# Three buffers of the fused layers moved to the lowest on-chip addresses

## The chip, the cores and the metric

The kernel runs on one core of a Trainium2 chip. A core has TensorE (PE, matrix products; its loads of stationary operands are listed as PEld), VectorE (DVE), ScalarE (ACT), GpSimd (POOL) and SyncE (SP), each with its own queue of instructions, worked off in order. Tiles live in the on-chip SBUF (128 partitions, so many bytes in each) and, for matrix products, in PSUM. The metric is the time of one execution in microseconds (us); lower is better.

## The reference

Sixteen graphs (batches) of 1024 nodes with 128 features pass through four layers. Each layer's output is added to its input and normalised over the features:

```
x = _layernorm(x + _L0_gnn_ref(x, adj, U))              # mean over neighbours, times U, relu
x = _layernorm(x + _L1_gnn_ref(x, adj, Wv, bv, ...))    # masked attention
x = _layernorm(x + _L2_gnn_ref(x, adj, W, a))           # four-headed graph attention
x = _layernorm(x + _L3_gnn_ref(x, adj, nodemask, ...))  # thinned links, three SAGE layers
```

Layer 3 first thins the links (`_dilate`, row by row), then runs three SAGE layers. Each of these gathers over the thinned links, divides every row by its length, and normalises each feature over all batches and nodes, so no SAGE layer can end before all 16 batches are through it. A linear map of the three results closes the layer.

## The kernel before, in words

`tile_gnn_stack` (L1494) calls two stages, one after the other in the program. A third, `general`, runs only if a flag says that the data is out of the usual, and did not run here.

**`fuse` (L185)** does layers 0 to 2 and the thinning for all batches. Its order of instructions is written by hand: `Loom` interleaves eleven sequences of steps by due times. Each batch's features live in `x0` (L656, three buffers of 4096 bytes a partition). The features are loaded there, all three layers update them in place, and after the last normalisation (`norm.apply`: a chain of small VectorE operations L621 to L635, then eight ScalarE operations L640) one DMA stores them from there to `x3` in DRAM (L1097). Layer 2's output is put together per head: the products `ps_b` (L1060) go through `sums` (L1066) into the totals `every` (L1021), by four VectorE operations (L1070, L1074, L1079, L1080). Then the totals are divided (L1084, L1086) and added to the features (L1089), and the statistics taken (L613). For the last batch this chain from L1070 to L1097 is the end of the stage.

**`sage` (L1111)** does the three SAGE layers and the closing map. Its order is not by hand: the framework orders each engine's instructions by itself, in program order where they are ready by its estimate, with later ones in the gaps. For this it may put `sage` instructions among the last ones of `fuse`. The first SAGE layer works through batches 1, 2, ..., 14, 0, 15, and for the first two of these ("first", "second"):

- `turned` (L1288) loads the features of one batch from `x3` to `xn`, turns them on TensorE (L1295) and copies them to `raw` (L1296, ScalarE).
- `fetch` (L1151) loads the eight blocks of thinned links, one byte an element, to `packed` (tile `ad`, L1155, 12 buffers).
- `weigh` (L1174) multiplies `raw` by the layer's weights `wr` (L1182) and splits the product in `z_hi` (ScalarE, L1184) and `z_lo` (VectorE, L1185).
- `spread_out` (L1158) casts a block of links from one byte to four: blocks 1 and 6 on VectorE (L1162), the six others on ScalarE (L1164), to `links` (12 buffers).
- `count` (L1194) sums the links of each node on TensorE against `ones_bf` (L1199) to `deg_c` (L1203); `degrees` (L1206) sends the sums through DRAM to `deg`; `own` (L1214) uses them.
- `gather` (L1187) is the large product, links by `z_hi` and `z_lo` (L1193). `mix` (L1219, L1222) ends it, with `settle` and `finish` behind.

An `ad` buffer is free for a later batch when its block has been cast and counted.

The weights `wr`, `wx` and vectors of layer 0 are loaded on POOL's queue (`matrix` L48, `column` L53) to the pool `sage_const`, which also holds `ones_bf` (written by VectorE, L1138) and, at its end, `piece`, `once` and `consts`.

**Addresses.** A pool takes a stretch of SBUF in the order in which the pools are opened, and the stretches are given back when a stage ends. So the pools of `sage` lie over those of `fuse`, and what is written first there has to wait until what was there is no longer used. Adding up the tiles (bytes a partition, counted from the start of `fuse_const`):

| pool of `fuse` | from | to | holds, among others |
|---|---|---|---|
| fuse_const | 0 | 6128 | identities, weights of layers 0 to 2 |
| fuse_1 | 6144 | 56576 | `both`, `py`, `ranked`, `qt`, `kt`, `vn`, `every`, `sums` |
| fuse_2 | 56576 | 135168 | `row`, `a`, `x0`, `pr`, `pieces` |
| fuse_3 | 135168 | 172800 | `src` and others, `has` |
| fuse_4 | 172800 | 206592 | `g`, `adt` and others |
| fuse_small | 206592 | 211168 | `ln_st`, `ln_t` and others |

| pool of `sage` | from | to | holds |
|---|---|---|---|
| sage_const | 0 | 7296 | `ones_bf`, weights, `piece`, `once`, `consts` |
| sage_raw | 7296 | 91008 | `raw`, `deg`, `deg_c`, `mf` |
| sage_links | 91008 | 140160 | `links` |
| sage_packed | 140160 | 152448 | `ad` |
| sage_1, sage_2 | 152448 | 207744 | `xn`, `z_hi`, `z_lo`, `own`, `o` and others |

Of the kernel before, what the change touches and what calls it, by code (L numbers as in the profile page):

```python
# [7 lines left out]
F32 = mybir.dt.float32  # L8
# [13 lines left out]
P = 128  # L22
# [162 lines left out]
def fuse(S, ctx, a, x3, adt_d, viol, B=16):  # L185
# [20 lines left out]
    tc, nc = S.tc, S.nc  # L206
# [4 lines left out]
    H, DH = a2.shape[0], a2.shape[1] // 2  # L211
# [4 lines left out]
    D1, GUESS = DH + 1, float(0x5F3759DF) + 3.5 * 2.0**23  # L216
# [3 lines left out]
    dps = ctx.enter_context(tc.tile_pool(name="fuse_dps", bufs=2, space=PSUM))  # L220
    dram = ctx.enter_context(tc.tile_pool(name="fuse_dram", bufs=1, space=DRAM))
    t_d = dram.tile([B, H, N], F32, name="t_d")
    p1 = ctx.enter_context(tc.tile_pool(name="fuse_1", bufs=1))
    p2 = ctx.enter_context(tc.tile_pool(name="fuse_2", bufs=2))
    p3 = ctx.enter_context(tc.tile_pool(name="fuse_3", bufs=3))
# [418 lines left out]
    def flip4(ps, blocks, q):  # L644
        for c in range(4):
            nc.tensor.transpose(ps[:, c, :], blocks(4 * q + c), ident)

    x01 = {}

    def layer0():  # L650
        for b in range(B):
            yield b, "features"
            if b >= 3:
                yield Step(None, 0.0, after=(f"stored {b - 3}",))
            yield Step("SP", 0.2, lag=5.0)
            x0 = x01[b] = p2.tile([P, 8, P], F32, name="x0", bufs=3)  # L656
            nc.sync.dma_start(x0, x_d[b].rearrange("(c p) d -> p c d", p=P))
            py = p1.tile([P, 8, 3 * P + 1], BF16, name="py")
            for q in range(2):
                s = slice(4 * q, 4 * q + 4)  # L660
                yield Step("PE", 0.45, take=[("one", "l0")])
                ps_f = one.tile([P, 4, P], F32, name="ps_f", tag="one")
                flip4(ps_f, lambda c: x0[:, c, :], q)
                yield Step("ACT", 0.47, give=[("one", "l0")])
                xt = p4.tile([P, 4, P], F32, name="xt0", tag="t2k", bufs=3)
                nc.scalar.copy(xt, ps_f)
                yield Step("PE", 0.89, take=[("one", "l0")])
                ps_y = one.tile([P, 4, P], F32, name="ps_y", tag="one")
                for c in range(4):
                    nc.tensor.matmul(ps_y[:, c, :], xt[:, c, :], u_w, start=True, stop=True)  # L670
                yield Step("ACT", 0.47)
                nc.scalar.copy(py[:, s, 0:P], ps_y)
                yield Step("DVE", 0.6, give=[("one", "l0")])
                d = p4.tile([P, 4, P], F32, name="d", tag="t2k", bufs=3)
                V.tensor_tensor(d, ps_y, py[:, s, 0:P], ALU.subtract)
                yield Step("ACT", 0.47)
                nc.scalar.copy(py[:, s, P : 2 * P], d)
                yield Step("DVE", 0.61)
                V.tensor_tensor(py[:, s, 2 * P : 3 * P], d, py[:, s, P : 2 * P], ALU.subtract)
                V.memset(py[:, s, 3 * P : 3 * P + 1], 1.0)  # L680
            yield b, "gather"
            norm = Norm(x0)
            rdeg = sm.tile([P, 8], F32, name="rdeg")
            for p in range(4):
                for k in range(2):
                    ib = 2 * p + k
                    for jb in range(8):
                        if jb % 4 == 0:
                            yield Step(
                                "PE", 0.68, after=(f"has {b} 7", None) if ib + jb == 0 else (),  # L690
                                take=[("one", "l0")] if k + jb == 0 else (),
                            )
                        if k + jb == 0:
                            ps_g = one.tile([P, 2, 256], F32, name="ps_g", tag="one")

                        for q, e in ((2, P + 1), (1, P), (0, P)):
                            nc.tensor.matmul(  # L697
                                ps_g[:, k, 0:e], has[b][:, jb, ib * P : (ib + 1) * P],
                                py[:, jb, q * P : q * P + e],
                                start=(jb == 0 and q == 2), stop=(jb == 7 and q == 0),  # L700
                            )
                s = slice(2 * p, 2 * p + 2)
                yield Step("DVE", 0.1)
                V.reciprocal(rdeg[:, s], ps_g[:, :, P])
                yield Step("ACT", 0.5, give=[("one", "l0")])
                y = p4.tile([P, 2, P], F32, name="y", tag="t2k", bufs=3)
                for k in range(2):
                    nc.scalar.activation(
                        y[:, k, :], ps_g[:, k, 0:P], AF.Relu, scale=rdeg[:, 2 * p + k : 2 * p + k + 1]
                    )  # L710
                yield Step("DVE", 0.86)
                V.tensor_tensor(x0[:, s, :], x0[:, s, :], y, ALU.add)
                norm.take(2 * p)
                norm.take(2 * p + 1)
            yield b, "norm 0"
            yield from norm.apply(f"x1 {b}")
# [295 lines left out]
    def layer2_sums():  # L1012
        for b in each:
            yield b, "sums"
            yield from outputs(b)

    def outputs(b):
        yield Step(None, 0.0, after=(f"bd {b}", f"end {b} 1"))
        x2 = x01.pop(b)
        _, side, pieces, bd = stuff[b]  # L1020
        every_t = p1.tile([P, 8 * H * D1], F32, name="every")  # L1021
        every = every_t.rearrange("p (c h d) -> p c h d", c=8, h=H)
        for jp in range(2):
            for u in range(4):
# [21 lines left out]
        for h in range(H):  # L1046
            for q in range(2):
                for jb in range(8):
                    if jb % 2 == 0:
                        yield Step(  # L1050
                            "PE", 0.72, after=(f"g {b} {h} {q}",), take=[("two", "b")] if q + jb == 0 else (),
                            mark=f"b {b} {h}" if q and jb == 6 else None,
                            give=[("g", (b, h, 0)), ("g", (b, h, 1))] if q and jb == 6 else (),
                        )
                    if q + jb == 0:
                        ps_b = two.tile([P, 2, 512], F32, name="ps_b", tag="two")
                    u, o = jb // 4, jb % 4 * 2 * D1
                    for k in range(4):
                        for t in range(3):
                            nc.tensor.matmul(  # L1060
                                ps_b[:, u, o : o + 2 * D1], side[h, q][:, k, jb * P : (jb + 1) * P],
                                pieces[:, 4 * q + k, :, h, t, :],
                                start=(q == 0 and jb % 4 == 0 and k + t == 0),
                                stop=(q == 1 and jb % 4 == 3 and k == 3 and t == 2),
                            )
            sums = p1.tile([P, 8, 2, D1], F32, name="sums")  # L1066
            up, rest, to = sums[:, :, 0, :], sums[:, :, 1, :], every[:, :, h, :]
            got = ps_b[:, :, 0 : 8 * D1].rearrange("p v (u k d) -> p k v u d", u=4, k=2)
            yield Step("DVE", 0.9, after=(f"b {b} {h}",), give=[("two", "b")])
            V.tensor_tensor(  # L1070
                up.rearrange("p (v u) d -> p v u d", v=2), got[:, 0],
                bd[:, 0, h, :].rearrange("p (v c) -> p v c", v=2).unsqueeze(3).to_broadcast([P, 2, 4, D1]), ALU.mult,
            )
            V.tensor_tensor(  # L1074
                rest.rearrange("p (v u) d -> p v u d", v=2), to.rearrange("p (v u) d -> p v u d", v=2),
                got[:, 1], ALU.subtract,
            )
            yield Step("DVE", 0.9)
            V.tensor_tensor(rest, rest, bd[:, 1, h, :].unsqueeze(2).to_broadcast([P, 8, D1]), ALU.mult)  # L1079
            V.tensor_tensor(to, up, rest, ALU.add)  # L1080
# [23 lines left out]
    with tc.manual_schedule():  # L1104
        loom.run(
            layer2_sums(), sides(), values(), layer2(), scores(), layer1(), layer0(), signs(batches),
            loads(batches), ranks(batches), dilate(batches),
        )
# [1091 lines left out]
```

## Time and profile before

| | us |
|---|---|
| runs of the kernel | 2831.93, 2835.9, 2838.47 (median 2835.9) |
| the profiled execution's own time | 2838.25 |
| its span in the profile | 2836.2 |
| busy in the span | PE 2671.0, PEld 2238.0, ACT 2234.9, DVE 2137.6, POOL 19.5 |

The stage change lies a little after two thirds of the span: the last `ps_b` product of `fuse` ends at 2042.4 us, and the first `ps_g` product of `sage` starts at 2063.7 us. In lines of the timeline the first two numbers are the start and the length in us, then come engine, line, operation, tiles (out <- in), the count, and in brackets the idle time before and what ended it. In lines of waits the numbers are the total in us, how often, and the longest.

### The profile page before, as it was taken

The page shows a single profiled execution, that of the slowest core. Times are in us where ns is not written, and L with a number is a line of the kernel's source. Part 1 is how long each engine was busy: PE and PEld are TensorE (multiplying, and loading weights), DVE is VectorE, ACT ScalarE, POOL GpSimd, SP SyncE. Part 2 cuts the span into 40 slices and gives each one's busy share as a digit, 9 for nine tenths or more (in the row PEclk, how much of TensorE's full clock was granted, in tenths as well). Part 3 has the DMA queues.
Part 4 walks back from the last instruction along what each step waited for, and adds up shares of the span by engine and source line. Part 5 has one row for each costly group of instructions (what it writes and reads, how often), then busy time and mean ns, then how long its engine had stood idle before and what let it go on. Part 6 is the DMA issues. An engine that isn't in the chain of part 4 may idle for free. (4 is left out here: it accounts for less than half of the span.)

```text
span 2836.2 us, 82907 instructions
## 1 busy us (share of the span) xinstructions
PE 2671.0 (94%) x35125; PEld 2238.0 (79%) x35125; DVE 2137.6 (75%) x5704; ACT 2234.9 (79%) x3351; POOL 19.5 (1%) x43
## 2 busy tenths in 40 slices
PE   5999999999999999999999999999799989989997
PEld 4778888888888888888888888877678767767787
DVE  6577777878788786877878687786457768868866
ACT  3788888888888888888888888888666668777625
POOL 1000000000000000000000000000100000000000
PEclk9999999999999999999999999999899989989999
DMA  5111231212303122130312203020355446455368
GB/s 186 44 40 60 63 113 36 95 56 67 106 17 113 39 91 80 43 106 27 109 40 84 94 29 113 24 84 10 92 150 156 146 150 195 137 170 178 117 224 267
DMA packets 225340, 280.26 MB, mean 99 GB/s; under 512 B 18360, under 2 KB 185120, under 8 KB 224960
## 3 DMA queue, kind: packets, MB, share of 16 engines
q1 hardware_dynamic: 223904, 273.69, 30.0%
q8 instruction: 277, 4.54, 0.7%
q0 software_dynamic: 1056, 1.19, 0.2%
q14 instruction: 103, 0.84, 0.1%
HBM read 224.01 MB, written 50.79 MB: 97 GB/s over the span
## 5 line engine op out<-in xcount | busy, mean ns | idle before, releaser
L880 ACT ACTIVATE g<-row,st 128x1024 int8<-128x1024 f32 x512 | 567.1, 1148 | 6.2 <-DMA row<-t_d 6.1
L1060 PE MATMUL ps_b<-pieces,g 128*128 128x66 bf16 x12288 | 422.8, 195 | 2.2 <-DVE g L887 2.2
L1060 PEld LDWEIGHTS <-g 128*128 128x128 fp8e4 x12288 | 403.6, 98 | 4.1 <-DVE g L887 2.3
L1164 ACT CAST links<-ad 128x1024 fp32r<-128x1024 fp8e4 x288 | 290.4, 1047 | 94.3 <-PE ps_g L1193 83.2
L374 DVE TENSOR_TENSOR_SCAN ranked<-has 128x1024 bf16<-128x1024 fp8e4 x128 | 291.6, 2282 | 0.0
L813 PE MATMUL ps_s<-qt,kt 128*128 128x512 f32 x512 | 277.8, 624 | 12.4 <-ACT pr L821 11.8
L456 ACT ACTIVATE x<-both,thr 128x1024 f16<-128x1024 bf16 (+7 forms) x384 | 277.3, 764 | 15.1 <-DVE part L471 8.3
L841 PE MATMUL ps_a<-vn,pr 128*128 128x129 f32 x2048 | 274.1, 281 | 0.0
L1193 PE MATMUL ps_g<-links,z_hi 128*128 128x512 f32 x768 | 260.7, 420 | 0.0
L1193 PE MATMUL ps_g<-links,z_lo 128*128 128x512 f32 x768 | 244.2, 400 | 0.0
L841 PEld LDWEIGHTS ps_a<-vn,pr 128*128 128x128 f32 x2048 | 243.9, 191 | 0.1
L697 PE MATMUL ps_g<-py,has 128*128 128x128 bf16 (+1 forms) x3072 | 205.6, 222 | 0.0
L887 DVE TENSOR_TENSOR g<-g,has 128x1024 int16<-128x1024 int16 x256 | 174.0, 685 | 37.0 <-ACT g L880 37.0
L1032 PE MATMUL ps_m<-pieces,has 128*128 128x132 bf16 x3072 | 196.4, 223 | 5.0 <-ACT pieces L994 3.8
L815 PEld LDWEIGHTS <-has 128*128 128x128 fp8e4 x1024 | 78.7, 98 | 146.0 <-issue 146.0
L1032 PEld LDWEIGHTS <-has 128*128 128x128 fp8e4 x3072 | 188.6, 97 | 6.1 <-issue 5.9
L821 ACT ACTIVATE pr<-ps_s,bound 128x1024 f32<-128x1024 f32 x128 | 141.6, 1106 | 62.0 <-PE ps_s L815 61.7
L697 PEld LDWEIGHTS <-has 128*128 128x128 fp8e4 x3072 | 184.2, 99 | 0.5
L640 ACT ACTIVATE x<-x,ln_t 128x128 f32<-128x128 f32 x384 | 154.6, 486 | 35.8 <-DVE ln_t L635 35.8
L598 ACT ACTIVATE adt<-ps_n 128x512 fp8e4<-128x512 f32 x256 | 152.1, 610 | 27.0 <-PE ps_n L589 23.8
L1193 PEld LDWEIGHTS ps_g<-links,z_lo 128*128 128x128 f32 x768 | 147.0, 192 | 33.1
L561 ACT ACTIVATE x<-ps_r,left 128x512 f16<-128x512 f32 (+1 forms) x192 | 110.2, 581 | 59.4 <-PE ps_r L543 59.0
(295 smaller groups left out, 5524.2 us busy)
## 6 DMA issues: line engine op xcount, KB each, us to landing
a<-in_adj_dram SPq DMA_DIRECT2D x130, 512.0 KB
ad<-adt_d SPq DMA_DIRECT2D x384, 128.0 KB
row<-t_d SPq DMA_DIRECT2D x64, 512.0 KB
row<-rn_d SPq DMA_DIRECT2D x45, 512.0 KB
adt_d<-adt SPq DMA_DIRECT2D x256, 64.0 KB
h_d<-raw SPq DMA_DIRECT2D x32, 512.0 KB
hl<-h_d SPq DMA_DIRECT2D x32, 512.0 KB
x<-in_x_dram SPq DMA_DIRECT2D x16, 512.0 KB
```

Of the source, the lines that this page charges most:

```text
L374: V.tensor_tensor_scan(ranked[c][r], has[c][:, r, :], links[c][:, r, EDGE - 1 : EDGE - 1 + N].bitcast(U8), 0.0, ALU.add, ALU.subtract,)
L456: nc.scalar.activation(x, both[:, at[r] : at[r + 1]], AF.Abs, bias=far[:, r : r + 1], scale=2.0)
L640: nc.scalar.activation(self.y[:, c, :], self.y[:, c, :], AF.Identity, bias=nb[:, c, :], scale=rs[:, c, :])
L697: nc.tensor.matmul(ps_g[:, k, 0:e], has[b][:, jb, ib * P : (ib + 1) * P], py[:, jb, q * P : q * P + e], start=(jb == 0 and q == 2), stop=( ...
L813: nc.tensor.matmul(ps_s[:, u, :], kt[:, at_j], qt[:, f : f + 512], start=True, stop=False)
L841: nc.tensor.matmul(ps_a[:, 0 : P + 1], made[b, i][:, u, ib % 4 * P : (ib % 4 + 1) * P], qkv[b][2][:, i % 4 * 2 + u, :], start=(i % 4 + u = ...
L880: nc.scalar.activation(sg[:, k, :].bitcast(I8), rows[b, h], AF.Sign, bias=st[:, 1, h, ib : ib + 1], scale=-1.0)
L887: V.tensor_tensor(sg.bitcast(I16), sg.bitcast(I16), has[b][:, 2 * q : 2 * q + 2, :].bitcast(I16), ALU.bitwise_and,)
L1032: nc.tensor.matmul(ps_m[:, u // 2, o : o + H * D1], has[b][:, ib, jb * P : (jb + 1) * P], pieces[:, ib, 1, :, t, :], start=(t == 0 and ib ...
L1060: nc.tensor.matmul(ps_b[:, u, o : o + 2 * D1], side[h, q][:, k, jb * P : (jb + 1) * P], pieces[:, 4 * q + k, :, h, t, :], start=(q == 0 an ...
L1164: A.copy(a, t.packed[jb])
L1193: PE.matmul(t.ps[f], z[:, jb, :], t.links[jb][:, halves[f]], start=(jb + i == 0), stop=False)
```

## The change

`x0`, `every` and `sums` get a pool of their own, `fuse_late`, opened ahead of `fuse_1` and so directly behind `fuse_const`. Number and size of their buffers stay (3 x 4096, 4224 and 2112 bytes). No instruction of `fuse` or `sage` is added, taken away or changed.

```diff
     t_d = dram.tile([B, H, N], F32, name="t_d")
+    late = ctx.enter_context(tc.tile_pool(name="fuse_late", bufs=1))
     p1 = ctx.enter_context(tc.tile_pool(name="fuse_1", bufs=1))
     p2 = ctx.enter_context(tc.tile_pool(name="fuse_2", bufs=2))
...
-            x0 = x01[b] = p2.tile([P, 8, P], F32, name="x0", bufs=3)
+            x0 = x01[b] = late.tile([P, 8, P], F32, name="x0", bufs=3)
...
-        every_t = p1.tile([P, 8 * H * D1], F32, name="every")
+        every_t = late.tile([P, 8 * H * D1], F32, name="every")
...
-            sums = p1.tile([P, 8, 2, D1], F32, name="sums")
+            sums = late.tile([P, 8, 2, D1], F32, name="sums")
```

By the same adding up, `fuse_late` lies from 6144 to 24768, `fuse_1` from 24768 to 68864 and `fuse_2` from 68864 to 135168. Everything behind stays where it was, and so do the pools of `sage`.

## The prediction

> **What bounds the kernel now.** The page's first part has PE busy 94% of the span, but the change adds no work and takes none away: it can act only where tiles of `sage` wait for tiles of `fuse`. So I read the stage change, first by windows. The columns are the stretch and its length, then busy us (and instructions) of PE, PEld, DVE, ACT and POOL, then the granted PE clock, the DMA share and GB/s.
>
> ```profile
> 2042.40:2058.00 15.60, 2.99 (x72) 2.65 (x72) 8.23 (x31) 3.25 (x9) 10.01 (x19) 0.62 0.71 211
> 2058.00:2063.70 5.70, 5.14 (x32) 5.12 (x32) 2.48 (x6) 5.55 (x8) 0.00 (x0) 0.55 0.36 94
> 2063.70:2081.00 17.30, 16.06 (x192) 12.44 (x188) 7.69 (x14) 14.35 (x19) 0.00 (x0) 1.00 0.61 177
> 2081.00:2097.00 16.00, 16.00 (x153) 12.79 (x152) 8.95 (x19) 10.25 (x14) 0.00 (x0) 0.89 0.48 132
> 2097.00:2111.40 14.40, 14.40 (x152) 11.51 (x151) 10.94 (x20) 9.24 (x13) 0.00 (x0) 1.00 0.51 157
> ```
>
> From the last `ps_b` product to 2058 PE has 2.99 us of work in 15.60. The first batch's stretch (17.30 us) has PE idle for 1.24 us; the third batch, undisturbed, takes 14.40. Then the timeline of the same place, for who releases whom:
>
> ```profile
> 2047.08 1.64 DVE L613 BATCH_NORM_STATS2 ln_st<-x 128x6 f32<-128x128 f32 x8
> 2047.71 0.55 POOL L48 DMA_DIRECT2D wr<-in_L_gnn_Wr_dram  x1 [2033.45 <-DVE x L1089]
> ...
> 2048.70 0.17 DVE L1138 MEMSET ones_bf<- 128x128 bf16 x1
> 2048.97 1.85 PE L1199 MATMUL ps_d<-ones_bf,ad 128*128 128x1 bf16 x64 [2.69 <-DMA ad<-adt_d]
> 2049.14 0.11 DVE L1472 MEMSET once<- 128x64 uint32 x1
> 2051.22 3.18 ACT L640 ACTIVATE x<-x,ln_t 128x128 f32<-128x128 f32 x8 [13.01 <-DVE ln_t L635]
> 2054.43 0.37 SPq L1097 DMA_DIRECT2D x<-x  x1
> 2057.93 1.07 ACT L1296 COPY raw<-ps_f 128x512 f32<-128x512 f32 x2 [3.53 <-DMA x<-x]
> 2058.15 0.23 DVE L1136 TENSOR_SCALAR mf<-never 128x128 f32<-128x128 f32 x1 [6.97 <-DMA x<-x]
> 2058.72 3.72 PE L1182 MATMUL ps_z<-wr,raw 128*128 128x128 f32 x16
> 2058.89 2.00 ACT L1164 CAST links<-ad 128x1024 fp32r<-128x1024 fp8e4 x2
> 2059.17 0.67 DVE L1162 CAST links<-ad 128x1024 fp32r<-128x1024 fp8e4 x1
> 2062.23 1.48 PE L1295 MATMUL ps_f<-ident,xn 128*128 128x128 f32 x8
> ```
>
> Two rules of the framework can be read here. **Waits go by pool, not by tile**: `mf` lies at byte 89,728, over a buffer of attention weights `pr` (last read by L841 at 1960.5), yet waits for the store of the features `x0`, which shares `fuse_2` with them; and `wr`, at byte 256, over constants, waits for L1089, the last reader of `every` in `fuse_1`, of which `sage_const` covers only bytes 6144 to 7296. **Gaps are filled**: the fills of `ones_bf` and `once` stand inside the last batch's VectorE chain, because they were ready there. Call T0 the landing of the feature store, 2057.9. Today `raw`, `mf` and all `links` start at T0, `wr` and `ones_bf` ten microseconds before it.
>
> **The change part by part.** *Instructions:* none is added or removed, and each tile of `fuse` keeps its number of buffers, so inside `fuse` no wait is new; address alone gets zero. The nearest rows: L1086 writes to `every` in `fuse_1` and L1089 to `x0` in `fuse_2`, both 128x1024 f32 from two inputs, and both took 1.23 us, so an address has no price that shows here.
>
> *`sage_links` (91,008 to 140,160)* lies over `fuse_2` and `fuse_3`. Without `x0` the last users of these are the `ps_b` products, which end at 2042.4, so casts may start there instead of at T0, as blocks land. PE's count of all eight blocks starts at 2048.97, so the last block lands by 2048.9. ScalarE is idle for 13.01 us there: six casts of 1.05 (2.00 for two overlapping) are 6.2 us and fit. This leaves the stretch behind T0 less full: the first batch's stretch is 17.30 against 14.40, so at most 2.9 us can come back. Only 1.24 of these are idle PE, and part of that waits for `ad` blocks whose buffers need the count too. I take 1.7, with ends 0 and 2.9.
>
> *The same casts on VectorE* do harm. Blocks 1 and 6 of the first batch and block 1 of the second (the 12 buffers reach so far) are 0.68 us each. By the gap filling just read they stand inside the chain L1070 to L635, which sets T0 and has no slack: 3 x 0.68 = 2.0 us later. Ends: 0 (they stay behind L635) and 6 (VectorE also stands still till a block lands, see the rivals). On ScalarE casts may push L640 by at most one of 1.05, inside these ends.
>
> *`sage_const` (0 to 7296)* now lies over `fuse_late` (from 6144), by 1152 bytes. By the pool rule all of it, `wr`, `wx` and `ones_bf` too, waits for T0 instead of L1089. The last reader ended at 2047.05 and POOL issued at 2047.71, 0.66 later. How long the load takes:
>
> ```profile
> wr<-in_L_gnn_Wr_dram POOLq DMA_DIRECT2D x3, 64.0 KB, 2.4
> ```
>
> So `wr` is there at T0 + 0.66 + 2.4 = T0 + 3.1, where `ps_z` starts today at 2058.72, T0 + 0.8: 2.3 us later. Behind `wr` on POOL stand the eighteen other loads of weights and vectors, 0.53 each to issue; `wx` and the first vector are needed at the first `mix` and `settle`, 15 us on. `ones_bf` at T0 + 0.3 moves the count (1.85 us of PE) from its free place at 2049 to behind T0, but into the hole in which PE waits for `wr`; the second batch's turn `ps_f` (1.48) may fill the rest. PE's work from T0 to the first `ps_g` is then 1.85 + 3.72 + 1.48 + 0.3 = 7.35 against 5.8 today, so the delay is at least 1.5, and at most 2.3 plus a slow load (the longest of L48's took 4.9, 2.5 more). I take 2.0, ends 1.5 and 4.8. The degree's way through DRAM (L1211, L1212) moves by as much and is needed only at the first `mix`, 15 us on; DVE's `own` waits 2.05 for it already, and the casts queued behind it are done by then.
>
> *`sage_raw`* lies over `fuse_late`, `fuse_1` and `fuse_2` alike: T0 as before. `ad`, `xn`, `z_hi` and the rest lie over pools that do not change. On SP's queue the store L1097 stays behind the same twelve `ad` loads, since a thirteenth needs the count.
>
> **Sum:** +2.0 (chain) +2.0 (weights and count) -1.7 (links) = +2.3 on the profiled execution's 2838.25 (span 2836.2 and 2.05 around it), so 2840.55. That execution lies 2.35 above the median of the runs, 2835.9, so on the median's scale the forecast is 2838.2, 0.08% up. A measurement of this kernel tells about 0.2% (5.7 us) from no change; the three runs alone spread over 6.5.
>
> One rule weighs on this. The granted clock is 0.50 to 0.62 while PE idles before T0 and 1.00 from 2064 on. The Trainium skill (TensorE: Matmul & The Clock Gate, "What's actually happening") has PE at half rate after an idle window of about 3.4 us and at full rate after about as long a busy one. By it the count, now directly ahead of `ps_z`, would begin the warming up earlier, and my 2.0 for weights and count would be nearer 1.5, if the hole for `wr` does not break the window. Another rule speaks for a loss: by SBUF — State Buffer, "SBUF: two separate sides", a copy or cast of VectorE in its two-port mode shuts GpSimd out of a shared port, and so holds up loads issued there. By it each cast of `links` still behind T0 could add its length to the wait for `wr`; no run here shows one.
>
> **The rivals.**
> 1. *The casts come early and nothing pays for them.* If the filled-in casts leave the chain alone and PE has work until `wr` lands, -2.9 + 1.5 remains, or down to -2.9: 2833.0 to 2834.5 on the median's scale. For it: ScalarE's 13.01 us of idling. Against it: `ones_bf` and `once` inside the chain, and the 1152 bytes.
> 2. *VectorE stands still for a block, slower.* The engine's order is fixed; a cast of block 6 put in behind L1084 (2044.5) would hold up the whole chain until the block lands, as late as 2048.9: 4.4, and 2.0 for the casts themselves: +6.4 in place of +2.0, the sum +6.7, so 2842.6. It decides from 3.4 us of standing still (5.7 - 2.3). For it: L1070 to L635 has no slack and blocks land late, PE waited 2.69 for them. Against it: the framework may know this and put the cast behind L613.
> 3. *The change does not do what it says:* some other tile in `fuse_2` or `fuse_3` holds `links` as long as before, and only the price of `sage_const` remains: +2.0, 2837.9. Against it: no reader of these pools after 2042.4 is in the trace.
>
> **How the numbers follow.** Forecast 0.48, rival 1 0.20, rival 2 0.22, rival 3 0.10. The range takes the forecast with its ends (-2.9 + 0 + 1.5 = -1.4, and up to +5 with one slow term), all of rival 1 and most of rival 2 and some of a median's own spread: 2831 to 2844. For faster by over 0.2% nothing reaches -5.7 but a reordering of the whole stage by the framework: 0.07. Slower by over 0.2%: rival 2 and the slow end of the weights, 0.23. Between: 0.70.
>
> **What would show it.** Right: L1164 on ScalarE between 2043 and 2051; L1162 among the operations L1079 to L635, the store's landing some 2 us later; POOL's first L48 and the `ones_bf` fill behind that landing, and PE's `ps_d` count with them; the first batch's stretch nearer 15.5 than 17.3. Wrong: `wr` still loaded at 2047.7, or no cast before T0. A time outside 2831 to 2844 would mean that the order of the whole stage has changed, or that addresses have a price after all.

## The result, and the profile after

The changed kernel's median is 2838.04 us (2833.92 to 2843.2, 21 runs), that of the kernel before, timed beside it, 2832.88 us (2827.36 to 2838.47, 21 runs). The two medians differ by 5.2 us. The ratio, which all comparisons below use, is 1.0016, with a 95% interval of 1.001 to 1.0022: some 4.5 us slower, with 2.8 to 6.2 inside the interval. The profiled execution after took 2840.76 us, its span 2838.9 (before: 2838.25 and 2836.2). Every line number behind the new pool's is one higher than before.

For the comparison I count from the start of the last batch's chain (the last `sums<-ps_b`), called c: 2042.44 before, 2041.37 after. T0 is again the start of `raw`, which the feature store releases. The windows after, cut at the same events as those of before, which the prediction shows (columns: the stretch and its length; busy us of PE, PEld, DVE, ACT and POOL; the granted PE clock; DMA share; GB/s):

```profile
2041.40:2060.80 19.40, 1.25 (x8) 0.86 (x8) 9.75 (x32) 11.81 (x18) 0.00 (x0) 0.59 0.47 141
2060.80:2068.90 8.10, 6.83 (x91) 6.44 (x92) 1.66 (x7) 2.24 (x4) 6.88 (x13) 0.50 0.53 153
2068.90:2084.70 15.80, 15.80 (x193) 13.24 (x192) 7.00 (x12) 9.30 (x12) 3.17 (x6) 1.00 0.68 204
2084.70:2099.10 14.40, 14.40 (x153) 11.68 (x152) 8.71 (x18) 10.80 (x15) 0.00 (x0) 1.00 0.43 123
2099.10:2113.50 14.40, 14.40 (x152) 11.50 (x151) 10.90 (x20) 9.23 (x13) 0.00 (x0) 1.00 0.53 157
```

The chain takes 19.40 us in place of 15.60 (ACT is busy in it for 11.81 in place of 3.25: casts of `links`), T0 to the first `ps_g` 8.10 in place of 5.70 (POOL now works here: the weights), and the next two batches 15.80 and 14.40 in place of 17.30 and 16.00. The first two lines lose 6.2 us, the next two give back 3.1. The third batch's last `mix` ends 72.13 us behind c; before it was 68.95: +3.2. Half of what is given back is the clock's: in the fourth line PE is busy all through in both kernels, but was granted 0.89 before and 1.00 here. The timeline says who waits (... stands for lines left out):

```profile
2041.72 0.42 DVE L1075 TENSOR_TENSOR sums<-every,ps_b 128x264 f32<-128x264 f32 x1
...
2044.62 8.62 ACT L1165 CAST links<-ad 128x1024 fp32r<-128x1024 fp8e4 x9 [7.50 <-DMA ad<-adt_d]
2045.04 0.69 DVE L1163 CAST links<-ad 128x1024 fp32r<-128x1024 fp8e4 x1 [2.90 <-DMA ad<-adt_d]
...
2045.65 0.43 DVE L1080 TENSOR_TENSOR sums<-sums,bd 128x264 f32<-128x264 f32 x1
...
2048.11 0.69 DVE L1163 CAST links<-ad 128x1024 fp32r<-128x1024 fp8e4 x1
...
2051.53 0.67 DVE L1163 CAST links<-ad 128x1024 fp32r<-128x1024 fp8e4 x1
...
2057.78 0.37 SPq L1098 DMA_DIRECT2D x<-x  x1
2060.79 1.07 ACT L1297 COPY raw<-ps_f 128x512 f32<-128x512 f32 x2 [3.04 <-DMA x<-x]
2060.82 0.23 DVE L1137 TENSOR_SCALAR mf<-never 128x128 f32<-128x128 f32 x1 [6.28 <-DMA x<-x]
2061.02 0.17 DVE L1139 MEMSET ones_bf<- 128x128 bf16 x1
...
2061.39 1.84 PE L1200 MATMUL ps_d<-ones_bf,ad 128*128 128x1 bf16 x64 [15.90 <-ACT raw L1297]
2061.46 0.55 POOL L48 DMA_DIRECT2D wr<-in_L_gnn_Wr_dram  x1 [2047.31 <-ACT raw L1297]
...
2064.29 0.25 PE L1200 MATMUL ps_d<-ones_bf,ad 128*128 128x1 bf16 x4 [0.37 <-DVE deg_rows L1211]
...
2064.40 3.76 PE L1183 MATMUL ps_z<-wr,raw 128*128 128x128 f32 x16
```

The three casts of VectorE stand inside the chain. The first of them, block 1, stands ahead of L1080 and waits 2.90 us for its block, and the whole chain with it. Behind T0 come `ones_bf`, the count and the loads of `wr` in the forecast's order; `ps_z` starts 3.6 us behind T0, 0.8 before.

### The profile page after: what moved, and what is told of

It is laid out like the page before. It is cut to its first block, busy times and chain, and to the rows that moved or that the text cites. A ratio compares the mean times of both kernels' runs of the same rounds, so it can differ in the third digit from the quotient of the medians.

```text
span 2838.9 us, 82916 instructions
## 1 busy us (share of the span) xinstructions
PE 2669.2 (94%) x35125; PEld 2236.8 (79%) x35125; DVE 2137.1 (75%) x5704; ACT 2235.6 (79%) x3351; POOL 19.6 (1%) x43
## 4 chain that ended last, share of the span: by engine, by line
PE 68%; DVE 16%; ACT 8%; DMA 4%; issue 2%; SPq 1%; ACTq 0%; DVEq 0%
PE ps_g L1194 12%; PE ps_b L1061 9%; PE ps_a L842 9%; PE ps_s L814 7%; DVE ranked L375 6%; PE ps_g L698 4%; PE ps_z L1183 3%; PE ps_r L544 3%; PE ps_g L1223 3%; ACT g L881 2%; PE ps_y L1420 2%; PE ps_s L816 2%; DVE g L888 2%; ACT x L457 2%; DMA row<-t_d 2%
## 5 line engine op out<-in xcount | busy, mean ns | idle before, releaser
L881 ACT ACTIVATE g<-row,st 128x1024 int8<-128x1024 f32 x512 | 566.9, 1148 | 6.8 <-DMA row<-t_d 6.7
L641 ACT ACTIVATE x<-x,ln_t 128x128 f32<-128x128 f32 x384 | 154.5, 486 | 24.1 <-DVE ln_t L636 24.1
```

Of the source, the lines that this page charges most:

```text
L641: nc.scalar.activation(self.y[:, c, :], self.y[:, c, :], AF.Identity, bias=nb[:, c, :], scale=rs[:, c, :])
L881: nc.scalar.activation(sg[:, k, :].bitcast(I8), rows[b, h], AF.Sign, bias=st[:, 1, h, ib : ib + 1], scale=-1.0)
```

## The experiments

Every kernel of the experiments was timed in five rounds beside the kernel before: 12 runs each, but 11 of both_mended_even and features_on_top_waits_by_tile, and 6 of sums_in_front. "c" and "third mix" are of the one profiled execution of each kernel. "Third mix" is the end of the third batch's last `mix`, counted from c, and "first mix" that of the first batch. The expectations count bytes from the start of a partition, 18,176 more than the tables of the pools above: `x0` began at 91,136 before and begins at 24,320 in the changed kernel.

| kernel | start of `x0` modulo 256 | median us | ratio to before (95%) | c | third mix |
|---|---|---|---|---|---|
| before | 0 | | | 2042.4 | 68.95 |
| after | 0 | 2838.04 | 1.0016 (1.001 to 1.0022) | 2041.4 | 72.13 |
| late_behind_fuse_1 | 64 | 2846.52 | 1.0035 (1.0024 to 1.0045) | 2049.7 | 69.32 |
| casts_behind_chain | 0 | 2833.61 | 0.9993 (0.9982 to 1.0005) | 2043.9 | 72.13 |
| both_mended | 64 | 2839.66 | 1.001 (0.9999 to 1.002) | 2050.0 | 65.36 |
| totals_sums_only | 0 | 2836.59 | 1.0001 (0.999 to 1.0012) | 2044.4 | 69.82 |
| both_mended_even | 0 | 2833.64 | 0.999 (0.9981 to 0.9999) | 2045.3 | 65.63 |
| sums_in_front | 192 | 2844.56 | 1.0035 (1.0023 to 1.0047) | 2048.1 | 70.10 |
| features_on_top_waits_by_tile | 0 | 2835.09 | 0.9999 (0.999 to 1.0008) | 2039.1 | 65.59 |
| on_top_by_tile_casts_behind_chain | 0 | 2832.52 | 0.9992 (0.9983 to 1.0002) | 2042.9 | 66.14 |
| late_behind_fuse_1_even | 0 | 2836.48 | 1.0007 (0.9998 to 1.0016) | 2044.4 | 69.27 |
| on_top_high_halves_first | 0 | 2831.3 | 0.9988 (0.9979 to 0.9997) | 2042.4 | 64.80 |

Three of the third mixes (before, casts_behind_chain, totals_sums_only) hold something that is no wait: within the second batch a stretch of 3.4 us in which PE was busy all through and was granted 0.50. In before (columns as above):

```profile
2090.40:2093.80 3.40, 3.40 (x16) 2.52 (x14) 1.21 (x5) 2.16 (x3) 0.00 (x0) 0.50 0.37 113
```

That batch takes 15.9 to 16.0 us in these three and 14.3 in the changed kernel, so 1.6 to 1.7 us of the third mix is the clock's; without it they are at 67.3, 70.5 and 68.1. Each profiled execution has two to six such stretches between 2080 and 2300 us, at batches that differ from kernel to kernel. What brings them on, no run here shows.

### First round: undo the weights' wait, the casts in the chain, both, and leave the features out

**late_behind_fuse_1**: the new pool is opened behind `fuse_1`, so that the weights no longer lie over it.

```diff
-    late = ctx.enter_context(tc.tile_pool(name="fuse_late", bufs=1))
     p1 = ctx.enter_context(tc.tile_pool(name="fuse_1", bufs=1))
+    late = ctx.enter_context(tc.tile_pool(name="fuse_late", bufs=1))
```

> The changed kernel with its new pool opened behind fuse_1 instead of ahead of it, so that sage_const no longer lies over the features. Theory (three terms in the stage change): the loads of wr and the fill of ones_bf run before the last batch's chain, the three VectorE casts stay inside the chain, the feature store still lands about 4 us late; of the changed kernel's loss the 2.4 us of weights and count go, and 0 to 3 us over the kernel before remain. Rival (addresses have a price inside the first stage): features, totals and sums still lie elsewhere than before, the loss stays at about 5 us. Rival (the whole order of the SAGE stage got worse): the loss stays, spread over the stage and not at its start.

**casts_behind_chain**: VectorE's casts are queued behind the last operation of the last batch's chain.

```diff
-            V.scalar_tensor_tensor(nb, both, -0.5, y, ALU.mult, ALU.mult)
+            S.chain_end = V.scalar_tensor_tensor(nb, both, -0.5, y, ALU.mult, ALU.mult)
...
-            V.tensor_copy(a, t.packed[jb])
+            with tc.issue_after(S.chain_end.ins):
+                V.tensor_copy(a, t.packed[jb])
```

> The changed kernel, with the VectorE casts of links ordered behind the last operation of the last batch's normalisation (order only, no wait). Theory: the chain runs without a gap again, so the feature store lands about 15.5 us after the last ps_b product as in the kernel before (19.4 in the changed one); wr still waits for the store. The 4 us of the chain go, 1 us under to 2 us over the kernel before remain. Rivals (addresses, or the order of the whole stage): about 5 us slower than before as the changed kernel.

**both_mended**: the two edits together.

> Both of the other two edits together: new pool behind fuse_1, VectorE casts behind the chain. Theory: only the gain of the early links is left, 1 to 4 us faster than the kernel before, the first SAGE product starting about 5.5 us after the landing of the store and the first batch's stretch near 15 us instead of 17.3. Rivals (addresses, or the order of the whole stage): not faster than before.

**totals_sums_only**: the changed kernel with `x0` back in `fuse_2`.

```diff
-            x0 = x01[b] = late.tile([P, 8, P], F32, name="x0", bufs=3)
+            x0 = x01[b] = p2.tile([P, 8, P], F32, name="x0", bufs=3)
```

> The changed kernel with the features x0 back in fuse_2; only totals and sums stay in the new pool. Theory: links wait for the store again (x0 shares fuse_2 with what lies under them), sage_const waits for L1089 as before, so all waits are those of the kernel before: 0, within 1.5 us. Rival (addresses have a price): totals and sums are read and written by most of the last chain's operations, and a part of the 5 us stays, 2 us or more slower than before.

*Measured.* Without `x0` the rest of the change moves nothing that shows (1.0001, to within some 3 us). Holding the casts does what it should to the chain; here is the timeline of casts_behind_chain:

```profile
2052.83 1.29 DVE L1164 CAST links<-ad 128x1024 fp32r<-128x1024 fp8e4 x2
...
2055.93 0.37 SPq L1098 DMA_DIRECT2D x<-x  x1
...
2058.97 0.23 DVE L1137 TENSOR_SCALAR mf<-never 128x128 f32<-128x128 f32 x1 [4.85 <-DMA x<-x]
...
2059.32 0.63 DVE L1164 CAST links<-ad 128x1024 fp32r<-128x1024 fp8e4 x1
...
2059.61 0.55 POOL L48 DMA_DIRECT2D wr<-in_L_gnn_Wr_dram  x1 [2044.78 <-DVE once L1474]
...
2061.94 3.75 PE L1184 MATMUL ps_z<-wr,raw 128*128 128x128 f32 x16
```

Two of the casts now stand behind the chain and the third behind the landing, and the store is issued 11.99 us behind c, exactly as before (16.41 in the changed kernel). The weights are as late as there. In the runs the edit is worth 0.0023 of the ratio. In its profiled execution nothing of this is left at the third mix (72.13). The second batch's work is placed ahead of the first `ps_g` (c + 27.34), and PE was granted 0.50 until 2074.7, 15.7 us behind the landing (8.1 in the changed kernel); so the first mix comes only 1.6 us earlier (c + 41.79 for 43.37), and the stretch at 0.50 in the second batch takes these. That execution took 2843.15 us, the longest of its twelve, so it need not be typical of the median.

Both kernels with the pool behind `fuse_1` went against what I expected: 10 and 3 us slower than before by the ratio (the second's interval just reaches 1), though both stage changes are shorter than in the changed kernel, and that of both_mended 3.6 us shorter than before's (1.9 without the stretch at 0.50). The time is lost ahead of c, which comes 7 to 8 us late: in the first stage, whose instructions did not change. It is lost in small amounts, where ScalarE waits for the attention rows that SP loads behind the store of `x0`. The group of that operation between 300 and 1950 us, in before, then in late_behind_fuse_1 (columns: busy us, mean ns | idle us just before it, and what ended it):

```profile
L880 ACT ACTIVATE g<-row,st 128x1024 int8<-128x1024 f32 x437 | 484.8, 1148 | 6.2 <-DMA row<-t_d 6.1
```

```profile
L881 ACT ACTIVATE g<-row,st 128x1024 int8<-128x1024 f32 x433 | 480.3, 1148 | 14.3 <-DMA row<-t_d 14.2
```

As long an operation (1148 ns), and 8.1 us more idling for the row. It reaches PE: the products `ps_n` of the thinning wait for what ScalarE copies out (`adt`) for 6.5 us more, again between 300 and 1950 us in before and here (us in total, how often, the longest):

```profile
PE ps_n L583 <- ACT adt L598: 20.6, 53, 1.1
```

```profile
PE ps_n L584 <- ACT adt L599: 27.1, 51, 2.0
```

From SP's issue of the row to its use is 5.58 us in before and 6.17 here (medians of the ten to twelve uses that waited). The row's own address is the same as in the changed kernel, where it is 5.57. What differs is `x0`: it begins at byte 68,416, 64 past a multiple of 256.

### Second round: the start of x0

**both_mended_even** and, in the third round, **late_behind_fuse_1_even** put the totals and sums in a pool ahead of the features, in both_mended and in late_behind_fuse_1; nothing but the order of these three tiles changes.

```diff
     p1 = ctx.enter_context(tc.tile_pool(name="fuse_1", bufs=1))
+    late_s = ctx.enter_context(tc.tile_pool(name="fuse_late_s", bufs=1))
     late = ctx.enter_context(tc.tile_pool(name="fuse_late", bufs=1))
...
-        every_t = late.tile([P, 8 * H * D1], F32, name="every")
+        every_t = late_s.tile([P, 8 * H * D1], F32, name="every")
...
-            sums = late.tile([P, 8, 2, D1], F32, name="sums")
+            sums = late_s.tile([P, 8, 2, D1], F32, name="sums")
```

> The edit of both_mended, with one more: the totals and sums in a pool of their own ahead of the pool of the features, so that the features begin at byte 74,752 (146 times 512) in place of 68,416 (64 past a multiple of 128); every other tile keeps its address. Theory (an uneven start of the features slows their store and load, and the row loads queued behind them on SP come late, some 0.6 us a batch): the row's way from its issue to ScalarE's use is back to 5.5 to 5.8 us (6.21 in both_mended), the last batch's chain starts at 2041 to 2045 us (2050.0 in both_mended), and with the stage change kept 3 to 4 us better than before the kernel is 1 to 6 us faster than before, ratio 0.998 to 0.9996. Rival (the price comes from another thing, such as the order of the pools): the chain still starts at 2049 to 2051 and the ratio stays at 1.000 to 1.002.

> The kernel of late_behind_fuse_1 with the totals and sums in a pool of their own ahead of the features, which so begin at byte 74,752 (146 times 512) in place of 68,416 (64 past a multiple of 128). The casts are not held, so VectorE still stands still for a block inside the last chain; the weights need not wait for the store. Theory (an uneven start of the features costs the first stage 6 to 8 us): chain start at 2041 to 2046 (2049.7 in late_behind_fuse_1), ScalarE's idling for the rows of g between 300 and 1950 us at 5 to 9 us (14.3), time 5 to 9 us under late_behind_fuse_1's ratio, so 1.0005 to 1.0018 of before. Rival (the two runs with late features differ for another reason): chain start at 2048 or later, ratio 1.003 to 1.0045.

**sums_in_front** does the same to the changed kernel, where it turns an even start into an uneven one (`late_s` and `late` ahead of `fuse_1`).

> The changed kernel, with the totals and sums in a pool of their own in front of the pool of the features: the features begin at byte 30,656 (64 past a multiple of 128) in place of 24,320 (256 past a multiple of 512), and the first weights of the next stage lie over the totals and not over the features. Theory (an uneven start of the features has a price in the first stage): the last batch's chain starts 6 to 8 us later than in the changed kernel (2041.4), at 2047 to 2050; the weights load behind the chain's last reader of the totals, so the stage change is 1 to 3 us shorter than the changed kernel's; in all 6 to 11 us slower than before, ratio 1.002 to 1.004. Rival (the start has no price): the chain starts at 2041 to 2044, and with weights on time the kernel is 0 to 3 us slower than before, ratio 1.000 to 1.001.

*Measured.* Three pairs, and the same sign in all. An even start took late_behind_fuse_1 from 1.0035 to 1.0007 (0.0028, 7.9 us) and both_mended from 1.001 to 0.999 (0.002, 5.7 us). An uneven one took the changed kernel from 1.0016 to 1.0035, although its stage change became 2.0 us shorter (0.0019, 5.4 us). The same group of ScalarE in late_behind_fuse_1_even, in both_mended and both_mended_even, and in the changed kernel and sums_in_front:

```profile
L882 ACT ACTIVATE g<-row,st 128x1024 int8<-128x1024 f32 x437 | 484.7, 1148 | 5.5 <-DMA row<-t_d 5.5
```

```profile
L881 ACT ACTIVATE g<-row,st 128x1024 int8<-128x1024 f32 x433 | 480.5, 1149 | 14.0 <-DMA row<-t_d 14.0
```

```profile
L882 ACT ACTIVATE g<-row,st 128x1024 int8<-128x1024 f32 x435 | 482.7, 1148 | 8.8 <-DMA row<-t_d 8.8
```

```profile
L881 ACT ACTIVATE g<-row,st 128x1024 int8<-128x1024 f32 x435 | 482.4, 1148 | 6.8 <-DMA row<-t_d 6.7
```

```profile
L882 ACT ACTIVATE g<-row,st 128x1024 int8<-128x1024 f32 x434 | 481.4, 1148 | 12.9 <-DMA row<-t_d 12.9
```

Even starts idle 5.5 to 8.8 us here (before 6.2), uneven ones 12.9 to 14.3. PE's wait of `ps_n` follows (19.7 to 22.0 us with an even start, 26.3 to 27.1 with an uneven one), and so does c: 2044.4 for 2049.7, 2045.3 for 2050.0, and 2048.1 for the changed kernel's 2041.4. The rival (another thing in the order of the pools) is out: in each pair only these three tiles move, and `every` and `sums`, which no DMA touches, keep their own starts modulo 256.

### Third line of trial: nothing that the next stage needs lies over x0

**features_on_top_waits_by_tile** opens the features' pool behind `fuse_4`, keeps totals and sums where they were, and lets the six pools of `sage` behind `sage_const` wait for the tiles that they cover. **on_top_by_tile_casts_behind_chain** adds the hold of casts_behind_chain.

```diff
     p4 = ctx.enter_context(tc.tile_pool(name="fuse_4", bufs=4))
+    late = ctx.enter_context(tc.tile_pool(name="fuse_late", bufs=1))
...
-    rawp = ctx.enter_context(tc.tile_pool(name="sage_raw", bufs=1))
-    big = ctx.enter_context(tc.tile_pool(name="sage_links", bufs=12))
+    rawp = ctx.enter_context(tc.tile_pool(name="sage_raw", bufs=1, reuse_waits="tile"))
+    big = ctx.enter_context(tc.tile_pool(name="sage_links", bufs=12, reuse_waits="tile"))
...
```

> The features in a pool behind fuse_4, at byte 212,480 (415 times 512), totals and sums where they were before, and the pools of the next stage wait for the tiles that they cover, not for whole pools. Theory (the stage change is set by what lies over the features and what waits for their store): raw and links no longer wait for the store; first product of the links 13 to 18 us behind the chain's start (21.25 before), 3 to 8 us faster than before by the third mixing product, ratio 0.997 to 0.999; casts of VectorE inside the chain may give 2 to 4 of it back. Rival (the features' store itself, or the loads behind it, sets the end whatever lies over them): first product at 21 us or later, ratio 0.999 to 1.001.

> The kernel of features_on_top_waits_by_tile, with VectorE's casts of links held behind the last batch's chain (L636). Theory: the chain is as long as before (store lands 15.5 us behind the chain's start), so 2 to 4 us better than without the hold, 4 to 10 us faster than before, ratio 0.9965 to 0.9985. Rival (the casts inside the chain cost nothing once nothing waits for the chain's end): within 1 us of the kernel without the hold.

*Measured.* `raw` is freed from the store, as the timeline of the first shows: it starts 9.5 us before the store is even issued.

```profile
2047.30 0.59 ACT L1298 COPY raw<-ps_f 128x512 f32<-128x512 f32 x1 [2.13 <-PE ps_f L1297]
...
2056.77 0.37 SPq L1099 DMA_DIRECT2D x<-x  x1
```

Yet the first `ps_g` comes only 1.1 us earlier than before (c + 20.15 for 21.25), and the gain at the third mix (3.4 us, 1.7 without the stretch at 0.50 in before) does not show in the runs (0.9999). With the hold it is c + 18.98 and 0.9992. Both gained less than expected. In that kernel the wait has only moved, from the store to ScalarE's queue:

```profile
2054.40 3.19 ACT L642 ACTIVATE x<-x,ln_t 128x128 f32<-128x128 f32 x8
2057.49 3.87 ACT L1167 CAST links<-ad 128x1024 fp32r<-128x1024 fp8e4 x4
2061.26 1.05 ACT L1187 CAST z_hi<-ps_z 128x512 fp32r<-128x512 f32 x2
...
2061.89 0.80 PE L1196 MATMUL ps_g<-links,z_hi 128*128 128x512 f32 x1 [3.86 <-ACT z_hi L1187]
```

PE is idle for 3.86 us for `z_hi`, whose product ended at 2055.7, while ScalarE works off four casts queued ahead of it. **on_top_high_halves_first** queues them behind it:

```diff
-        A.copy(t.hi[:, s, :], ps_z)
+        S.high = A.copy(t.hi[:, s, :], ps_z)
...
+        elif t.n == 0 and t is first and jb >= 3:
+            with tc.issue_after(S.high.ins):
+                A.copy(a, t.packed[jb])
```

> The kernel of on_top_by_tile_casts_behind_chain, with ScalarE's casts of the first batch's blocks 3, 4, 5 and 7 queued behind its two copies of z_hi. There four casts (3.87 us) stood ahead of the z_hi that PE waited 3.86 us for. Theory (ScalarE's order now sets the first product of the links): first product 15 to 17.5 us behind the chain's start in place of 18.98, third mixing product 1 to 3 us earlier than 66.14, 1 to 3 us faster than that kernel, ratio to before 0.998 to 0.999. Rival (the casts are then late for the products, or PE's other work fills the stretch anyway): third mixing product at 66 us again, ratio 0.999.

*Measured*, in its timeline:

```profile
2058.92 1.08 ACT L1190 CAST z_hi<-ps_z 128x512 fp32r<-128x512 f32 x2
...
2059.87 2.96 ACT L1168 CAST links<-ad 128x1024 fp32r<-128x1024 fp8e4 x3
...
2060.80 1.20 PE L1199 MATMUL ps_g<-links,z_hi 128*128 128x512 f32 x2
```

The first `ps_g` starts 18.38 us behind c, not the 15 to 17.5 expected, since two copies of the second batch's `raw` went in ahead of `z_hi` on ScalarE (the second at 2058.44), and eight of its `ps_z` products ahead of `ps_g` on PE (from 2059.08); the third mix is 1.3 us earlier, as expected. The ratio of 0.9988 is the lowest of the study, 3.4 us under before with an interval of 0.9 to 6.0 us. Against the kernel without this edit (0.9992) the intervals overlap, so the step itself is shown in the trace and not in the runs.

## Why the prediction was right, and where it was not

The forecast was 2838.2 us, +2.3 and inside 0.2%; measured are 2838.04 us beside a before of 2832.88, so +4.5 (1.0016). That the time itself is met to 0.2 us is luck: the kernel before came out 3.0 us faster in 21 runs than in the three that the forecast stood on, and the change cost 2.2 more than forecast. "Within 0.2%" held by 0.04%, with an interval that reaches 1.0022, and the sum was half of what came. Its terms can now be taken one by one from the third mix of four even kernels: before 68.95 (67.3 without the stretch at 0.50); both_mended_even 65.63 (only what comes back early); late_behind_fuse_1_even 69.27 (with the casts in the chain); after 72.13 (with the weights too). The steps between them add up to the whole by construction, each comes from single executions, and other tiles lie elsewhere in these kernels, so each is a size and no exact part:

- **Links early: forecast -1.7, measured -1.6** (65.63 - 67.3; by the first mix, 36.68 for 38.52, it is -1.8). In the changed kernel ScalarE took nine casts in its hole, not six; the first batch's stretch is 15.80 for 17.30. The second batch's 16.00 before was no wait that the links could shorten: the prediction's own row has PE busy for all of it at a granted clock of 0.89, which its "1.00 from 2064 on" passes over.
- **Chain: forecast +2.0, measured +3.6** (69.27 - 65.63); in the changed kernel itself c to T0 grew by 3.93 (19.42 for 15.49). The casts cost about what was forecast: 0.6 each to the next operation, 1.8 in all. The step that failed is the one in which the forecast left the standing still to rival 2 alone and counted 0 for it: VectorE stood 2.90 us for block 1, behind L1075, not for block 6 behind L1084. The other direction is 0.3 us of smaller gaps (a fill that left the chain is part of it) and 0.5 of a store that landed sooner (3.04 for 3.53). It is rival 2's mechanism at another place, and it stays under the 3.4 us from which that rival was to decide.
- **Weights and count: forecast +2.0, measured +2.9** (72.13 - 69.27); `ps_z` starts 2.8 us later behind T0. The load was forecast rightly: POOL issued 0.67 us behind T0, and the first `wr`, the one that `ps_z` needs, took 2.2 us (forecast 2.4):

```profile
wr<-in_L_gnn_Wr_dram POOLq DMA_DIRECT2D x1, 64.0 KB, 2.2
```

So it was there at T0 + 2.9, and `ps_z` started at T0 + 3.6. What was mis-sized is the hole into which the count was to fit: the count, its turned sums and their copy `deg_rows` last until 2064.24, and four counts of the second batch, which wait for that copy, stand ahead of `ps_z` in PE's queue. In casts_behind_chain, where they stand behind it, `ps_z` starts 0.1 us behind the landing.
- **Sum at the third mix: +3.2** as profiled, +4.9 without the stretch at 0.50 in before (-1.6 + 3.6 + 2.9), beside +4.5 (2.8 to 6.2) in the runs. The forecast's gain was right, and its two costs were too small by 1.6 and 0.9. The runs have the same steps with wider bounds: 0.999, 1.0007 and 1.0016 are -2.8, +4.8 and +2.5 us, each uncertain by some 3 us. The fourth corner, casts_behind_chain (0.9993), makes the chain 6.5 us and the weights 0.9, so the runs alone do not tell the weights' price from nothing.

The rule on the clock that the prediction weighed would have made the weights cheaper. Here PE was granted 0.50 until 2068.9, 8.1 us behind T0 (before: until 2063.1, 5.2 behind it). In both that is 4.6 us behind the start of work without a hole (2064.29 and 2058.55). The count ended at 2063.2, and two holes of 0.3 and 0.4 us followed, which fits the prediction's own condition that the hole breaks the window. The rule on VectorE's copies and GpSimd shows no price, in a weak test: in casts_behind_chain a cast overlaps POOL's issue of `wr` by 0.34 us, and the issue (0.55) and the load (2.2) take as long as in the changed kernel.

Rival 1 (nothing pays for the early casts) is out, since both prices are there. Rival 3 (the change does nothing for `links`) is out by the nine casts at 2044.62.

**"An address has no price" was true of this change and wrong as a statement.** It rested on one pair of VectorE rows of 1.23 us. VectorE and ScalarE show none: with an even and an uneven start alike, L1090 on `x0` takes 1.22 us and L641 0.49. But DMA does, in three of the kernels built around the change. That the change itself was spared is luck: its `x0` happens to begin at 95 times 256.

## What to carry to other kernels

When tiles move between pools, list for each tile of the next stage what lies under it before and after, and whose last use it will wait for. Where the framework fills gaps, a tile that becomes free early may put an instruction that waits for a DMA inside a chain without slack, so hold it behind the chain's end. Look at the start of every tile that a DMA stores, and try it at a multiple of 256 bytes, above all where other transfers queue behind it (shown here for one tile). And a shorter stage change is worth measuring against c: what a layout gives at one place it can take in small amounts ahead of it. Where two single executions are compared, read the granted clock of each stretch first: here it was 1.7 us of a difference of 3.2.

## What the runs showed of the hardware

The tile `x0`, in rows of 512 bytes that one DMA loads and another stores, costs time when it begins off a multiple of 256 bytes: with `x0` at 64 or 192 past one the kernel lost 5.4 to 7.9 us over sixteen batches, and the rows loaded behind its store came some 0.5 us later (6.17 to 6.22 us from issue to use, against 5.57 to 5.77). A start of 256 past a multiple of 512, as in the changed kernel, has no price that shows.

It is the store that pays. From 0.5 to 2.5 us behind its issue the core's DMA moves 286 or 287 GB/s in all nine kernels with an even start and 245 in all three with an uneven one, at 64 and at 192 alike (medians of the thirteen stores between 300 and 1950 us). Here is the same batch in before and in late_behind_fuse_1:

```profile
880.85:882.85 2.00, 1.61 (x21) 1.13 (x19) 1.97 (x6) 2.00 (x7) 0.00 (x0) 1.00 0.96 289
```

```profile
882.47:884.47 2.00, 1.61 (x21) 1.13 (x19) 1.87 (x6) 2.00 (x7) 0.00 (x0) 1.00 0.78 245
```

The first 1024 packets of 512 bytes behind the store's issue, as many as it has, have all started after 2.33 or 2.34 us in the nine and 2.63 or 2.64 in the three: 0.3 of the 0.5 us. Behind the load of `x0` no such split shows (2.64 to 2.86 us in the nine, 2.73 to 2.80 in the three). The packets' own times differ too, but give no price: of the 52,640 packets of 512 bytes between 300 and 1950 us, 48,700 took 27 ns and some 70 took 41 with an even start (before, after, both_mended_even, late_behind_fuse_1_even); with an uneven one (late_behind_fuse_1, both_mended, sums_in_front) 39,400 to 39,900 took 27 and some 1,300 took 41, with a mean of 27.7 to 28.2 ns for 27.4.

The Trainium skill (DMA: Bandwidth & Descriptors, "How a descriptor splits into AXI transactions") says that a descriptor that does not start at a multiple of 256 bytes begins with a transaction from the boundary below, whose unused bytes are fetched and cost too. That agrees with which starts paid here and which did not. How large it is, the runs alone say. Where the rest of the 0.5 us arises, and whether other tiles would do the same, was not tried and stays open.
